# A graph layer on one core: dense work dealt by another rule, ending one group of 16 chunks later

## The chip, the cores and the metric

The kernel runs on one core of a Trainium2 chip. The time is device microseconds of one execution; lower is better. A time is the median of several runs, and a profile is one further execution with the profiler on.

## The reference

```python
h = jnp.maximum(_layernorm(x, axis=-1), 0.0)           # x: 12500 nodes x 128
xs = h[src]                                            # 200000 edges, sorted by dst
msgs = zeros
for i in range(4):                                     # four edge types
    msgs += where(edge_type == i, xs @ W[i] + b[i], 0)
return x + segment_sum(msgs, dst, num_segments=12500)
```

Each of the 200,000 edges takes the normalized row of its source node, multiplies it by the weights of the edge's type and adds the result to the row of its destination. The edges are sorted by destination, and the low destinations have by far the most edges.

## The kernel before, in words

The 200,000 edges are cut into 1,563 chunks of 128. They are treated in two ways.

*The first 568 chunks are dense.* Their edges go to some 1,700 destinations. For these the kernel counts, with matmuls of one-hots, how many edges of each type lead from each source node to each destination (`count`), and then multiplies the table of all 12,500 normalized rows by these counts (`multiply`). Up to 31 units of three destinations make a batch, and there are 19 batches, the first of 22. Counting a batch takes a matmul for each slot (`pt<-o,o`, L1099; 1,069 slots in all), for which VectorE makes two one-hots (L1066 and L1074), and ScalarE takes the sums out (L1107). Multiplying is called a pass: it reads the table in 33 blocks of three by 128 rows (`hs`, loaded on SyncE's queue into five buffers, L1195) and issues matmuls into `pa` (L1211). The first pass reads the table `htab`, with three parts for each row and three matmuls for 128 rows, and writes a packed table `dtab` on the way (`keep`, L1181 to L1183). Every later pass reads `dtab` with two matmuls for 128 rows, one of which needs counts that ScalarE has decoded (`dec`, L1167). While batch n is counted, batch n - 1 is passed over, a little behind.

*The other 995 chunks are sparse.* A gather on GpSimd's queue (L591) fetches the 128 source rows of a chunk from `htab`, VectorE makes a one-hot of key and type (`oh`, L609), and three matmuls of L644 add the rows up. A group is 16 chunks; once for a group, counts and sums are weighed with the weights (`weigh`, L661 to L670), and VectorE adds the outcome to a ring of destinations (L733), from which finished blocks are put out (`put_out`, `leave`, L766 and L771). The first three groups (RAW) are treated apart, from rows of `x`; their last steps (`raw_steps`, L702 to L715) are popped in group 3. Groups 3 to 59 have 16 chunks each, and 8, 12, 8, 4 and 3 chunks follow as groups 60 to 64. The gathers of group g + 1 are issued in group g, into ten buffers of two chunks, so a gather can run at most 20 chunks ahead of TensorE.

*The order on the engines is written out by hand* for TensorE, VectorE and ScalarE. In the main loop `sum_up` yields eight times in a group, after every two chunks, and at each yield dense steps are issued until their share of the whole reaches `pace(gi, part)`:

```python
for j, part in enumerate(sum_up(t0, g, *now, gi >= FULL)):
    while work and spent < pace(gi, part):
        spent = next(work, None)
```

`pace` gives every group the same number of columns, sparse columns (`columns`) and dense ones together. The dense total is the sum over slots and passes of estimated columns; `dense_work` adds up the same estimates as steps are issued. In the group in which the dense work is found to be over, its buffers are released, the finished rows of the dense destinations are fetched and leave in the group behind it (`leaves`), the blocks that are due from that group on are fetched ahead as well (`late`), and the sums are checked (`check_all`, which multiplies by an all-ones tile). `FULL` is 60, `LEAD` is 3, `NB` is 392.

Of the kernel before, what the change touches and what calls it, by code (L numbers as in the profile page):

```python
# [35 lines left out]
F32 = mybir.dt.float32  # L36
BF16 = mybir.dt.bfloat16
# [7 lines left out]
ALU = mybir.AluOpType  # L45
# [5 lines left out]
P = 128  # L51
EPS = 1e-5
UN = 3
G = 16
SG = 4
WIN = 32
# [10 lines left out]
SETTLE = 0.5  # L67
# [5 lines left out]
LEAD = RAW  # L73
# [4 lines left out]
DECS = 4  # L78
UP = 4096.0
PARTS = 2.05  # L80


@with_exitstack
def kernel(
# [10 lines left out]
    nc = tc.nc  # L95
    N, D = x.shape
    E = src.shape[0]
    NT, _, DO = w.shape
    assert D == P and DO == P
    NW = -(-N // P)  # L100
# [41 lines left out]
    for k in range(max(segs[0][4])):  # L142
        for s in (0, 1, 2, 3) if k == 0 else (1, 0, 2, 3):
            n = sum(c > k for c in segs[s][4])
# [9 lines left out]
    FULL = (TM - sum(ends_in)) // G  # L154
# [13 lines left out]
    alone = [(k, d) for k in range(0, max(segs[0][4]), 2) for d in range(FIRST) if segs[0][4][d] > k]  # L168
# [10 lines left out]
    batches = []  # L179
# [15 lines left out]
    def slots_of(u):  # L195

        got = []
        u = list(zip(u, (1.0, 256.0, 65536.0)))
        if u[0][0] is not None and u[0][0][1] >= FIRST:
            d = u[0][0][1]  # L200
            size = size_of(d)
            got += [(slot_at(k, d), None) for k in range(chunks_of(d, size))]
            del u[:size]
        for v, by in u:
            if v is not None:
                k, d = v
                got += [(slot_at(i, d), by) for i in (k, k + 1) if i < segs[0][4][d]]
        return got

    NSLOTS = sum(len(slots_of(u)) for vs in batches for u in vs)  # L210
    NB = NW * NT


# [209 lines left out]
    nc.gpsimd.iota(iota_i, pattern=[[1, P]], base=0, channel_multiplier=0)  # L423
    iota_b = const.tile([P, P], BF16, name="iota_b")
    nc.vector.tensor_copy(iota_b, iota_i)
    iota_1 = const.tile([P, P], BF16, name="iota_1")
    nc.vector.tensor_single_scalar(iota_1, iota_b, 1.0, op=ALU.add)
    iota_f = prep.tile([P, KR], F32, name="iota_f", bufs=1)
    nc.vector.tensor_copy(iota_f, iota_i[:, :KR])
    iota_d = prep.tile([P, NB], I32, name="iota_d", bufs=1)  # L430
# [19 lines left out]
    nc.vector.memset(ones_h, 1.0)  # L450
    ones_b = const.tile([P, 3], BF16, name="ones_b")
    nc.vector.memset(ones_b, 1.0)
    ones = const.tile([P, P], F32, name="ones")
    nc.vector.memset(ones, 1.0)
    eps = const.tile([P, 1], F32, name="eps")

    zero = const.tile([P, 1], F32, name="zero")
# [103 lines left out]
    marks = []  # L561
# [88 lines left out]
    def weigh(t0, g, oh, sb, last):  # L650
        win = window_of(C0 + t0)

        def bank(own):
            settle(owed)
            to = y_ps.tile([P, G * WIN], F32, name="py") if own else x_ps.tile([P, G * WIN], F32, name="pt")
            return to[:, : G * win].rearrange("p (g n) -> p g n", g=G)

        ohv = oh.rearrange("p g (t n) -> p g t n", t=NT)
        pc = bank(False)
        for t in range(NT):  # L660
            nc.tensor.matmul(  # L661
                pc[t * CG : (t + 1) * CG, :g, :], three, ohv[:, :g, t, :], start=True, stop=True, tile_position=(0, t * CG)
            )
        cnt = spool.tile([P, G * WIN], BF16, name="cnt", bufs=1)[:, : G * win].rearrange("p (g n) -> p g n", g=G)
        nc.scalar.copy(cnt[:, :g], pc[:, :g])  # L665
        yield True
        py = bank(not last)
        nc.tensor.matmul(py[:, :g, :], b128, cnt[:, :g, :], start=True, stop=False)
        for t in range(NT):
            nc.tensor.matmul(py[:, :g, :], wsb[:, t, :], sb[0][:, :g, t, :], start=False, stop=(t == NT - 1))  # L670
        adds.extend(ring_adds(t0, g, lambda i: py[:, i, :], win))
        yield True
# [174 lines left out]
    def check_all():  # L847
        nc.vector.tensor_single_scalar(bad[:, 4:5], most, MANY + 0.5, op=ALU.is_gt)
        many = const.tile([P, 3], F32, name="many")
        nc.vector.tensor_reduce(many[:, 0:1], bad, AX.X, ALU.add)  # L850
        nc.vector.tensor_copy(many[:, 1:2], seen)
        nc.vector.tensor_copy(many[:, 2:3], held)
        pb = x_ps.tile([P, 3], F32, name="pt")
        nc.tensor.matmul(pb, ones, many, start=True, stop=True)
        sums_ok = const.tile([P, 3], F32, name="sums_ok")
        nc.vector.tensor_single_scalar(sums_ok[:, 0:1], pb[:, 0:1], 0.5, op=ALU.is_gt)
        nc.vector.tensor_single_scalar(sums_ok[:, 1:2], pb[:, 1:2], 3.0 * E0, op=ALU.not_equal)
        nc.vector.tensor_single_scalar(sums_ok[:, 2:3], pb[:, 2:3], float(E0), op=ALU.not_equal)
        nc.vector.tensor_reduce(flag, sums_ok, AX.X, ALU.max)
# [14 lines left out]
    def make_slots(dix):  # L874
# [44 lines left out]
        for u0, n, _, _, caps in segs:  # L919
            i = 0  # L920
# [52 lines left out]
        def unpack(a, z, shared):  # L973
# [5 lines left out]
            marks.append(nc.vector.tensor_copy(hkT[:, a:z], hk).ins)  # L979
            lo = dix.tile([P, 512], I32, name="lo")[:, :n]  # L980
            nc.vector.tensor_single_scalar(lo, xi, 255, op=ALU.bitwise_and)
            marks.append(nc.vector.tensor_copy(loT[:, a:z], lo).ins)
            if shared:
                by = byT[:, a - FIRST : z - FIRST]
                nc.vector.tensor_single_scalar(xi, xi, 768, op=ALU.bitwise_and)
# [56 lines left out]
    def count(now, room):  # L1042
# [18 lines left out]
        def make(n):  # L1061
            at = before + n
            o1 = op1.tile([P, SLOTS, P], BF16, name="o1")
            o2 = o2s[:, at % SETS]
            for k, (i, s, by, first, last) in enumerate(sets[n]):
                one = nc.vector.tensor_scalar(o2[:, k, :NB], iota_n, hkT[:, s : s + 1], None, ALU.is_equal)  # L1066
                if k == 0 and at >= SETS:
                    held_by(one, released[at - SETS], "a set of slots has been counted as a whole")
                if by == 1.0:
                    one = nc.vector.tensor_scalar(o1[:, k], iota_1, loT[:, s : s + 1], None, ALU.is_equal)  # L1070
                else:
                    if by is None:
                        by = byT[:, s - FIRST : s - FIRST + 1]
                    one = nc.vector.tensor_scalar(o1[:, k], iota_1, loT[:, s : s + 1], by, ALU.is_equal, ALU.mult)  # L1074
                yield o1[:, k], o2[:, k], one.ins

        making = []
# [183 lines left out]
    def columns(gi):  # L1261

        K = NT * window_of(C0 + starts[gi])
        return sizes[gi] * (3 * max(64, K) + 5 * K)

    def pace(gi, part):

        last = FULL - 1
        if gi >= last:
            return 2.0  # L1270
        own = [columns(i) for i in range(LEAD, last)]
        a_group = (dense_columns() + sum(own)) / len(own)
        n = gi - LEAD
        if n < 0:
            return 0.0
        return ((n + part) * a_group - sum(own[:n]) - part * own[n]) / dense_columns()

    def dense_columns():
        return NSLOTS * float(NB) + sum(3 * len(vs) * (PARTS if i else 3.0) for i, vs in enumerate(batches)) * NW * NT

    def begin(n):
        now = [batches[n], None]
# [2 lines left out]
    def dense_work():  # L1285


        a_slot = float(NB)
        alone_slot = 3.5 * NB
        a_node = NW * NT  # L1290
        total = dense_columns() + sum(len(slots_of(u)) for u in batches[0]) * (alone_slot - a_slot)
        gone = 0.0
        before = None
        coming = None
        for n, vs in enumerate(batches + [None]):
            steps, led = {}, {}
            now = None
            if n == 1:
                end_raws()
            if vs:  # L1300
                now, first = coming or begin(n)
                coming = None
                steps[first] = sum(len(slots_of(u)) for u in vs) * (a_slot if before else alone_slot)
            if before:
                passed = multiply(before)
                steps[passed] = 3 * len(before[0]) * a_node * (PARTS if before[0] is not batches[0] else 3.0)
                led = {passed: SETTLE if before[0] is batches[1] else BEHIND}
            done = {st: 0.0 for st in steps}
            opened = 0 if before else DECS - 1
            while done:  # L1310
                while opened < DECS - 1 and (
                    vs is None or done.get(first, 1.0) >= led[passed] - BEHIND * (DECS - 1 - opened) / (DECS - 1)
                ):
                    next(passed)
                    opened += 1
                st = min(done, key=lambda st: done[st] + led.get(st, 0.0))
                part = next(st, None)
                if part is None:
                    del done[st]
                    gone += steps[st]  # L1320
                    if vs and st is first and n + 1 < len(batches):
                        coming = begin(n + 1)
                        next(coming[1])
                else:
                    done[st] = part
                    yield (gone + sum(done[st] * steps[st] for st in done)) / total
            before = now
        settle(sds)

# [308 lines left out]
    with tc.If(rv > 0):  # L1638
        with tc.tile_pool(name="slow", bufs=1) as slow, tc.tile_pool(name="slow_ps", bufs=1, space=PSUM) as slow_ps:
# [7 lines left out]
            nc.gpsimd.iota(part_i, pattern=[[0, 1]], base=NW * P + P, channel_multiplier=1)  # L1647
            part_f = slow.tile([P, 1], F32, name="part_f")
            nc.vector.tensor_copy(part_f, part_i)
            before = slow.tile([P, P], F32, name="before")  # L1650
            nc.gpsimd.affine_select(
                out=before, in_=ones, compare_op=ALU.is_gt, fill=0.0, base=0, pattern=[[1, P]], channel_multiplier=-1
# [106 lines left out]
```

## Time and profile before

| | |
|---|---|
| median of 3 runs | 1355.36 us (1352.13 to 1356.22) |
| the profiled execution | 1360.44 us |
| its span in the profile | 1358.7 us |
| busy: PE, ACT, DVE, POOL | 1243.1, 1066.8, 999.0, 977.8 us |
| gathers L591 | 947 |
| dense matmuls: L1211, L1099 | 3822, 1069 |

PE is TensorE, PEld its weight loads, ACT ScalarE, DVE VectorE, POOL GpSimd and SP SyncE. Rows by stretch hold, for each engine, the busy time and the number of instructions, then the granted share of TensorE's clock, the share of time in which the DMA engines were busy, and the rate in GB/s.

### The profile page before, as it was taken

Reading aid. Unit: us, or ns where it says so; the run is one execution under the profiler, and the core shown is the slowest. Engines: PE = TensorE matmul, PEld = TensorE weight load, DVE = VectorE, ACT = ScalarE, POOL = GpSimd, SP = SyncE. Lnnn points to the kernel's source line nnn. Section 1 sums busy time; section 2 is a strip of 40 time slices with the busy share of each in tenths; the row PEclk is TensorE's granted clock in tenths of the full one; section 3 lists DMA queues with packets and bytes.
Section 4 is the critical chain, followed back from the end, with each engine's and each line's share of the span. In section 5 each row is a group of like instructions: output and inputs, shape, how many; then the busy total and the mean of one; then the engine's idle time right before and its main releaser. Section 6 shows DMA issues by size and latency. Waiting matters only on the chain.

```text
span 1358.7 us, 30461 instructions
## 1 busy us (share of the span) xinstructions
PE 1243.1 (91%) x9232; PEld 872.8 (64%) x9232; DVE 999.0 (74%) x5139; ACT 1066.8 (79%) x1815; POOL 977.8 (72%) x1024
## 2 busy tenths in 40 slices
PE   5888877999999999999999999999999999998964
PEld 1445654777677766777777676666676666666743
DVE  8996568868888897888776867677676758773552
ACT  6887544889889888898988988888897978886710
POOL 7637463777777777777777777777777777777774
PEclk8885887999999999999999999999999999999977
DMA  7653596888788888888888888887877878778842
GB/s 243 216 204 86 176 338 216 244 272 266 243 256 259 250 255 241 249 257 265 256 259 254 267 249 257 248 246 246 273 227 238 265 214 261 235 234 281 267 122 62
DMA packets 184630, 322.56 MB, mean 237 GB/s; under 512 B 30243, under 2 KB 82524, under 8 KB 184460
## 3 DMA queue, kind: packets, MB, share of 16 engines
q1 hardware_dynamic: 132716, 214.63, 49.0%
q0 software_dynamic: 46992, 96.30, 26.0%
q10 hardware_dynamic: 4752, 9.64, 1.8%
q8 instruction: 73, 1.20, 0.4%
q14 instruction: 97, 0.79, 0.2%
HBM read 294.78 MB, written 25.67 MB: 236 GB/s over the span
## 4 chain that ended last, share of the span: by engine, by line
PE 65%; DMA 12%; DVE 6%; ACT 6%; issue 6%; POOL 4%; DVEq 0%; SPq 0%; ACTq 0%; POOLq 0%
PE pa L1211 35%; PE pt L1099 9%; PE py L670 7%; DMA hm<-htab,srcT 7%; PE ps L644 5%; POOL hm L591 4%; DMA dtab<-dec 2%; DMA hs<-dtab 2%; ACT dec L1167 2%; PE pt L1235 2%; ACT counts L1107 1%; PE ps L702 1%; DVE o L1074 1%; DVE o L1066 1%; PE pt L952 1%
## 5 line engine op out<-in xcount | busy, mean ns | idle before, releaser
L591 POOL DMA_INDIRECT hm<-htab,srcT x947 | 924.3, 976 | 342.1 <-issue 202.5
L1167 ACT ACTIVATE dec<-counts 128x1116 fp32r<-128x1116 uint8 (+1 forms) x594 | 672.2, 1152 | 9.9 <-PE pa L1211 9.0
L1066 DVE TENSOR_SCALAR o<-iota_n,hkT 128x392 bf16<-128x392 f16 x1069 | 354.4, 331 | 180.2 <-PE pt L1099 177.4
L1211 PE MATMUL pa<-dec,hs 128*128 128x372 f32 x1764 | 480.8, 380 | 0.0
L1211 PE MATMUL pa<-counts,hs 128*128 128x372 fp8e4 (+1 forms) x2058 | 435.0, 324 | 22.6 <-DMA hs<-htab 13.8
L1211 PEld LDWEIGHTS pa<-dec,hs 128*128 128x128 f32 x1764 | 309.5, 188 | 41.6 <-issue 0.5
L1107 ACT CAST counts<-pt 128x396 int32<-128x396 f32 x580 | 285.5, 510 | 50.1 <-PE pt L1099 26.2
L1099 PE MATMUL pt<-o,o 128*128 128x396 bf16 x1069 | 285.9, 342 | 15.8 <-ACT counts L1107 9.5
L1211 PEld LDWEIGHTS <-hs 128*128 128x128 f16 (+1 forms) x2058 | 189.6, 98 | 143.1 <-issue 19.4
L644 PE MATMUL ps<-oh,hm 128*128 128x72 bf16 (+7 forms) x2841 | 186.9, 201 | 32.3 <-DMA hm<-htab,srcT 30.9
L1074 DVE TENSOR_SCALAR o<-iota,loT,byT 128x128 bf16<-128x128 bf16 x647 | 216.3, 334 | 0.0
L733 DVE TENSOR_TENSOR ring<-ring,py 128x18 f32 (+6 forms) x912 | 159.0, 174 | 73.1 <-PE py L670 24.1
L644 PEld LDWEIGHTS <-hm 128*128 128x128 f16 x2841 | 136.9, 100 | 103.9 <-DMA hm<-htab,srcT 41.4
L634 ACT ACTIVATE sb<-ps 128x288 f32<-128x288 f32 (+8 forms) x237 | 101.8, 430 | 126.3 <-PE py L670 101.3
L609 DVE TENSOR_SCALAR oh<-iota_b,keyT 128x72 bf16<-128x72 bf16 (+7 forms) x947 | 163.0, 260 | 25.6 <-PE ps L644 24.4
L670 PE MATMUL py<-sb,wsb 128*128 128x288 f32 (+6 forms) x456 | 121.1, 409 | 0.0
L1099 PEld LDWEIGHTS <-o 128*128 128x128 bf16 x1069 | 80.4, 99 | 60.6 <-issue 17.5
L1074 DVE TENSOR_SCALAR o<-iota,loT 128x128 bf16<-128x128 bf16 x422 | 116.7, 277 | 0.0
L670 PEld LDWEIGHTS py<-sb,wsb 128*128 128x128 f32 x456 | 83.3, 193 | 20.7 <-issue 0.3
L575 POOL DMA_INDIRECT hx<-in_x_dram,srcT x48 | 48.0, 1001 | 23.8 <-issue 9.5
L665 ACT CAST cnt<-pt 128x288 bf16<-128x288 f32 (+10 forms) x62 | 25.5, 412 | 39.5 <-PE pt L661 33.6
L509 ACT ACTIVATE h<-hm,nmrt,rstdt 128x128 f32<-128x128 f32 x98 | 42.1, 489 | 0.9 <-DVE mvt L492 0.8
(250 smaller groups left out, 717.8 us busy)
## 6 DMA issues: line engine op xcount, KB each, us to landing
hs<-dtab SPq DMA_DIRECT2D x576, 288.0 KB
hm<-htab,srcT POOLq DMA_INDIRECT x947
htab<-h SPq DMA_DIRECT2D x32, 288.0 KB
hs<-htab SPq DMA_DIRECT2D x32, 288.0 KB
dtab<-dec ACTq DMA_DIRECT2D x32, 288.0 KB
xo<-in_x_dram SPq DMA_DIRECT2D x23, 256.0 KB
out_dram<-xo SPq DMA_DIRECT2D x23, 256.0 KB
hm<-in_x_dram SPq DMA_DIRECT2D x18, 192.0 KB
```

The lines of the kernel that those rows point to most:

```text
L591: one = nc.gpsimd.indirect_dma_start(out=hm[:, (i - h0) * D3 : (i - h0 + 1) * D3], out_offset=None, in_=htab, in_offset=bass.IndirectOffse ...
L609: nc.vector.tensor_scalar(oh[:, i, :], iota_b[:, :K], keyf[:, at : at + 1], None, ALU.is_equal)
L634: nc.scalar.activation(sb[0][:, i0:i1].rearrange("p g t n -> p g (t n)"), ps[:, : i1 - i0, :], AF.Copy, scale=1.0 / UP)
L644: nc.tensor.matmul(ps[:, i - i0, :], rows(i, c), oh[:, i, :], start=(c == 0), stop=(c == 2))
L670: nc.tensor.matmul(py[:, :g, :], wsb[:, t, :], sb[0][:, :g, t, :], start=False, stop=(t == NT - 1))
L733: nc.vector.tensor_tensor(to, to, of(i), ALU.add)
L1066: one = nc.vector.tensor_scalar(o2[:, k, :NB], iota_n, hkT[:, s : s + 1], None, ALU.is_equal)
L1074: one = nc.vector.tensor_scalar(o1[:, k], iota_1, loT[:, s : s + 1], by, ALU.is_equal, ALU.mult)
L1099: one = nc.tensor.matmul(pb, o1, o2, start=first, stop=last)
L1107: lambda i=i, pb=pb: nc.scalar.copy(counts[:, :, i * NT : (i + 1) * NT], pb.rearrange("p (b t) -> p b t", t=NT))
L1167: nc.scalar.activation(decoded[n][:, : j1 - j0, :nv].rearrange("p j (m v) -> p j m v", m=3), by_digit[:, j0:j1, : nu * NT * 4].rearrange(" ...
L1211: nc.tensor.matmul(to if c == 1 and not first else to.rearrange("p (m v) -> p m v", m=3), left, right, start=(j == 0 and c == 0), stop=(js ...
```

## The change

`pace` and `dense_work` now use the same two estimates, written as functions of how much of a step is done. A slot of the first batch, and of the first half of batch 2 (which is counted with no pass beside it), stands for 3.5 times the columns of another slot (`ALONE`). In the old rule only `dense_work` knew this, and for the first batch alone. The first pass stands for 4.4 instead of 3.0 columns for a node and unit (`FIRST_PASS`); the later ones keep 2.05. Group 3, with the steps of the raw groups, counts as 20,000 columns fuller (`RAW_WORK`; the sparse columns of a group are some 7,000 to 12,000). The dense work is dealt over groups 3 to 59 instead of 3 to 58 (`last`). Three smaller edits go with it: the constant `iota_1` is gone, and `loT` holds the value less one instead; the all-ones tile is made where it is used, not at the start; and `cnt` has room for 26 columns a chunk instead of 32.

```diff
+FIRST_PASS = 4.4
+ALONE = 3.5
+RAW_WORK = 20000.0
...
-    iota_1 = const.tile([P, P], BF16, name="iota_1")
-    nc.vector.tensor_single_scalar(iota_1, iota_b, 1.0, op=ALU.add)
...
-    ones = const.tile([P, P], F32, name="ones")
-    nc.vector.memset(ones, 1.0)
...
-        cnt = spool.tile([P, G * WIN], BF16, name="cnt", bufs=1)[:, : G * win].rearrange("p (g n) -> p g n", g=G)
+        cnt = spool.tile([P, G * KM // NT], BF16, name="cnt", bufs=1)[:, : G * win].rearrange("p (g n) -> p g n", g=G)
...
         pb = x_ps.tile([P, 3], F32, name="pt")
+        ones = outp.tile([P, P], F32, name="ones", bufs=1)
+        nc.vector.memset(ones, 1.0)
         nc.tensor.matmul(pb, ones, many, start=True, stop=True)
...
-            marks.append(nc.vector.tensor_copy(loT[:, a:z], lo).ins)
+            marks.append(nc.vector.tensor_single_scalar(loT[:, a:z], lo, -1.0, op=ALU.add).ins)
...
-                    one = nc.vector.tensor_scalar(o1[:, k], iota_1, loT[:, s : s + 1], None, ALU.is_equal)
+                    one = nc.vector.tensor_scalar(o1[:, k], iota_b, loT[:, s : s + 1], None, ALU.is_equal)
...
     def pace(gi, part):
 
-        last = FULL - 1
+        last = FULL
         if gi >= last:
             return 2.0
-        own = [columns(i) for i in range(LEAD, last)]
+        own = [columns(i) + (RAW_WORK if i == LEAD else 0.0) for i in range(LEAD, last)]
...
+    def counting_columns(n, part):
+
+        alone = 1.0 if n == 0 else SETTLE if n == 2 else 0.0
+        return sum(len(slots_of(u)) for u in batches[n]) * NB * (part + (ALONE - 1.0) * min(part, alone))
+
+    def passing_columns(n, part):
+        return 3.0 * len(batches[n]) * (PARTS if n else FIRST_PASS) * NW * NT * part
+
     def dense_columns():
-        return NSLOTS * float(NB) + sum(3 * len(vs) * (PARTS if i else 3.0) for i, vs in enumerate(batches)) * NW * NT
+        return sum(counting_columns(n, 1.0) + passing_columns(n, 1.0) for n in range(len(batches)))
...
-        a_slot = float(NB)
-        alone_slot = 3.5 * NB
-        a_node = NW * NT
-        total = dense_columns() + sum(len(slots_of(u)) for u in batches[0]) * (alone_slot - a_slot)
+        total = dense_columns()
...
-                steps[first] = sum(len(slots_of(u)) for u in vs) * (a_slot if before else alone_slot)
+                steps[first] = lambda part, n=n: counting_columns(n, part)
...
-                steps[passed] = 3 * len(before[0]) * a_node * (PARTS if before[0] is not batches[0] else 3.0)
+                steps[passed] = lambda part, n=n: passing_columns(n - 1, part)
...
-                    yield (gone + sum(done[st] * steps[st] for st in done)) / total
+                    yield (gone + sum(steps[st](done[st]) for st in done)) / total
```

More of the change, by code (lines that the diff above doesn't have):

```diff
@@ L208, in slots_of @@
         return got
-    NSLOTS = sum(len(slots_of(u)) for vs in batches for u in vs)
     NB = NW * NT
@@ L1073, in make @@
                         by = byT[:, s - FIRST : s - FIRST + 1]
-                    one = nc.vector.tensor_scalar(o1[:, k], iota_1, loT[:, s : s + 1], by, ALU.is_equal, ALU.mult)
+                    one = nc.vector.tensor_scalar(o1[:, k], iota_b, loT[:, s : s + 1], by, ALU.is_equal, ALU.mult)
                 yield o1[:, k], o2[:, k], one.ins
@@ L1319, in dense_work @@
                     del done[st]
-                    gone += steps[st]
+                    gone += steps[st](1.0)
                     if vs and st is first and n + 1 < len(batches):
@@ L1649 @@
             nc.vector.tensor_copy(part_f, part_i)
+            ones = slow.tile([P, P], F32, name="ones")
+            nc.vector.memset(ones, 1.0)
             before = slow.tile([P, P], F32, name="before")
```

## The prediction

> **What bounds the kernel now.** I read the page first, for span, chain and slices.
>
> ```profile
> span 1358.7 us, 30461 instructions
> ...
> POOL 7637463777777777777777777777777777777774
> ...
> PE 65%; DMA 12%; DVE 6%; ACT 6%; issue 6%; POOL 4%; DVEq 0%; SPq 0%; ACTq 0%; POOLq 0%
> ```
>
> The chain of waits names PE for 65% of the span. The POOL slices say something else: the same digit from the eighth slice to the last but one, whatever PE does. An engine that is fed by others does not run so evenly. To decide, I cut the span at the groups of 16 chunks that the loop walks through, at the first L644 matmul of a group, and asked for the busy times of each stretch (columns: length; busy time and count of PE, PEld, DVE, ACT, POOL; granted clock; DMA share; GB/s).
>
> ```profile
> 112.10:152.10 40.00, 33.32 (x201) 25.70 (x201) 21.41 (x96) 30.36 (x85) 23.59 (x25) 0.63 0.26 72
> 152.10:176.30 24.20, 20.72 (x194) 15.91 (x193) 18.49 (x84) 12.10 (x31) 15.78 (x15) 0.93 0.92 311
> 176.30:206.60 30.30, 22.36 (x195) 16.13 (x193) 17.56 (x79) 13.40 (x33) 17.20 (x18) 0.89 0.98 342
> 206.60:243.20 36.60, 28.54 (x173) 17.17 (x172) 31.48 (x152) 18.94 (x38) 15.52 (x15) 0.72 0.62 196
> 243.20:282.10 38.90, 38.27 (x314) 27.86 (x311) 29.47 (x165) 35.91 (x51) 29.71 (x31) 1.00 0.89 276
> 282.10:718.30 436.20, 427.30 (x3416) 309.54 (x3415) 356.03 (x1853) 384.63 (x608) 332.55 (x341) 1.00 0.84 255
> 718.30:1288.80 570.50, 548.23 (x4149) 390.59 (x4147) 398.29 (x2077) 478.25 (x729) 433.60 (x450) 1.00 0.82 251
> 1288.80:1344.80 56.00, 36.14 (x241) 24.80 (x240) 21.80 (x120) 7.47 (x18) 42.59 (x45) 0.71 0.40 106
> 1344.80:1358.70 13.90, 5.17 (x41) 3.98 (x39) 4.00 (x19) 1.17 (x3) 0.00 (x0) 0.75 0.13 37
> ```
>
> These are groups 3, 4, 5, 6, then 7 and 8, then 9 to 30, 31 to 58, and 59 to 64, and the rest after the last gather. The matmuls of L644 (three for each chunk, 48 for a group) show the cut: 22 groups, then 28.
>
> ```profile
> 282.10:718.30 436.20, 59.79 (x1057) 45.21 (x1058) 1.00 0.84 255
> 718.30:1288.80 570.50, 93.72 (x1344) 67.14 (x1343) 1.00 0.82 251
> ```
>
> From 282.1 to 1288.8 POOL issues 341 + 450 = 791 gathers in 1006.7 us, one in **1.273 us**, so 20.4 us for a group. In the stretch without dense work, 1288.8 to 1344.8, it is 56.0/45 = 1.24 us: hardly faster, with PE busy 65% and the DMA share halved. So POOL paces the kernel by itself from 282 on, and the end is its last gather plus 13.9 us. PE needs 427.3/22 = 19.4 us of work for a group, 98% of its stretch, then 548.2/28 = 19.6 us: it is just under POOL's pace.
>
> Before 282.1 POOL does lose time: 25 + 15 + 18 + 15 + 31 = 104 gathers take 170.0 us, where 104 x 1.273 = 132.4 would do. **37.6 us** are lost, and who took them stands in the waits of 112 to 282:
>
> ```profile
> POOL hm L591 <- PE ps L644: 25.7, 12, 5.0
> ...
> POOL hm L591 <- PE pt L1099: 12.7, 10, 3.4
> ```
>
> 38.4 us in 22 waits for PE. The row buffers hold 20 chunks; a gather waits until PE has multiplied the chunk 20 places earlier, and PE is late because dense work is queued between the sparse matmuls. That is the place the change touches.
>
> **The change part by part.** *Where the dense work goes.* Dense matmuls of the trace in these stretches, passes (L1211), then counts (L1099):
>
> ```profile
> 112.10:152.10 40.00, 2.24 (x18) 1.73 (x18) 0.63 0.26 72
> 152.10:176.30 24.20, 17.27 (x119) 11.57 (x117) 0.93 0.92 311
> 176.30:206.60 30.30, 18.05 (x119) 11.59 (x117) 0.89 0.98 342
> 206.60:243.20 36.60, 12.11 (x61) 7.61 (x60) 0.72 0.62 196
> 243.20:282.10 38.90, 30.49 (x162) 20.91 (x162) 1.00 0.89 276
> 282.10:718.30 436.20, 287.96 (x1486) 197.83 (x1484) 1.00 0.84 255
> 718.30:1288.80 570.50, 360.56 (x1864) 247.91 (x1864) 1.00 0.82 251
> ```
>
> ```profile
> 112.10:152.10 40.00, 9.69 (x28) 2.81 (x28) 0.63 0.26 72
> 152.10:176.30 24.20, 4.28 (x12) 1.20 (x12) 0.93 0.92 311
> 176.30:206.60 30.30, 4.67 (x13) 1.34 (x13) 0.89 0.98 342
> 206.60:243.20 36.60, 12.94 (x41) 3.63 (x41) 0.72 0.62 196
> 243.20:282.10 38.90, 7.38 (x30) 1.88 (x28) 1.00 0.89 276
> 282.10:718.30 436.20, 124.32 (x493) 34.74 (x493) 1.00 0.84 255
> 718.30:1288.80 570.50, 122.59 (x455) 34.75 (x454) 1.00 0.82 251
> ```
>
> I worked the rule of `pace` through by arithmetic, step by step. With the old constants it gives 18, 117, 117, 60 and 72 + 90 passes and 28, 12, 13, 41 and 24 + 4 counts for groups 3 to 8, which is what these rows show. With the new ones it gives 0, 54, 90, 81, 69, 0 passes and 13, 19, 9, 9, 9, 27 counts, and from group 9 to 59 some 69 passes and 19 counts in each; the last pass ends with group 59, not 58.
>
> *Group 3.* It loses 15 counts and 18 passes. The passes are 2.2 us. A count is worth 0.35 us by PE's row (9.69/28). VectorE, which must first make two one-hots for it, needs 0.33 + 0.33 us:
>
> ```profile
> L1066 DVE TENSOR_SCALAR o<-iota_n,hkT 128x392 bf16<-128x392 f16 x1069 | 354.4, 331 | 180.2 <-PE pt L1099 177.4
> ...
> L1074 DVE TENSOR_SCALAR o<-iota,loT,byT 128x128 bf16<-128x128 bf16 x647 | 216.3, 334 | 0.0
> L733 DVE TENSOR_TENSOR ring<-ring,py 128x18 f32 (+6 forms) x912 | 159.0, 174 | 73.1 <-PE py L670 24.1
> ...
> L609 DVE TENSOR_SCALAR oh<-iota_b,keyT 128x72 bf16<-128x72 bf16 (+7 forms) x947 | 163.0, 260 | 25.6 <-PE ps L644 24.4
> ```
>
> So 15 counts are 5.2 to 10.0 us; the other work of this group, which goes through ACT (30.4 of 40.0 us busy) as well, stays. I take 40 - 9 = 31 us, nearer to PE's row: group 4 starts at 143 and not at 152. If ACT holds the group up, nothing but 2 us goes.
>
> *Groups 4 to 7.* The old groups 4 and 5 took 54.5 us for 238 passes with everything that lay among them: 0.229 us for a pass. At that price 90, 81 and 69 passes are 20.6, 18.5 and 15.8 us; 54 passes are 12.4 us, and with 9 counts made alone at 0.665 us and 10 beside passes at 0.25 us (124.32/493), group 4 is 20.9 us. All are at or under POOL's 20.4, so POOL sets them: 4 x 20.4 = 82. The price holds a DMA share of 0.92 to 0.98; spread over four groups the first pass asks for less, so it is no lower bound. Its loads on SP's queue and its stores on ACT's move along with it; both queues lose by it, since the same bytes have longer.
>
> *Group 8.* 27 counts alone on VectorE, 27 x 0.665 = 18.0 us, and beside them 16 one-hots at 0.26 and 16 additions to the ring at 0.174: 25 us on VectorE. Group 9 then starts at 143 + 82 + 25 = 250 where it was 282.1: **32 us** earlier, and POOL, which is 20 chunks ahead in both, as well. It would be 37.6 if POOL never waited.
>
> *From group 9 on.* 51 groups take 983 counts and 3,528 passes, where 50 took 947 and 3,348: 0.33 counts and 2.2 passes more for a group. By these rows a count is 0.25 us and a pass 0.194 us, so PE needs 0.51 us more: 19.9 us for groups 9 to 30, 20.1 from 31 on, against POOL's 20.4. PE's idle time there that is not waiting for a gather (8.9 us in 22 groups, 0.4 for each) stays: 20.3 and 20.5. That is even with POOL. It costs between nothing and 0.3 us for a group; I take 2 us in all.
>
> *The end.* After group 59 come 35 chunks, 44.6 us at POOL's pace, in which PE is busy two thirds. The tables' final rows leave one group later, in group 61, still covered by POOL's gathers there; the output block due at group 59 is now loaded when it is put out instead of ahead, and its load waits for a buffer. On VectorE the additions to the ring and the next one-hots are queued behind that. It costs nothing as long as VectorE catches up within 20 chunks; without that cover it is bounded by the gathers of the group it lies in, 12 x 1.273 = 15 us.
>
> *The constant.* One 128x128 constant less, the comparison shifted by one in `loT` (an instruction changed, none added), the all-ones tile filled later, a smaller `cnt`: a few instructions of a fraction of a microsecond each, beside POOL's pace. Nothing.
>
> The sum against the profiled execution: 1360.4 - 32 + 2 = 1330. The runs shown have their median 5.1 us below it (1355.4), so **1325** for the median.
>
> **Rivals.** *PE becomes the bound after group 9.* For: 98% busy, an estimate that comes out even. Against: its stretch 718 to 1288 still had 22 us idle. At 0.3 us over POOL, 51 groups give back 15: 1340.
>
> *PE's clock falls in the thin groups.* Granted clock and PE's busy share go together in the rows: 1.00 at 98%, 0.72 at 78%, 0.71 at 65% (1288.8 to 1344.8). The thinned groups would have PE busy some 16 of 20 us. At a clock of 0.5, 20.72 us of group 4 before, scaled to 90 passes of 119 and from 0.93 to 0.5, are 29 us: groups 4 to 8 take about 130 us, group 9 starts near 273, and 9 us are gained: 1346. The page "TensorE: Matmul & The Clock Gate" of the Trainium skill, Part 1, states a rule against this change: the clock is halved by default and after an idle window of about 3.4 us, and only sustained activity restores it. The rows between 0.63 and 0.93 agree with a mix of the two. By that rule spreading matmuls thinner is not free.
>
> *Slower: PE's queue gets longer than POOL's pace hides.* If a group of 9 to 59 took x us, group 59 ends at 250 + 51x, and 15 gathers, those beyond the 20 that the buffers hold, and the tail follow, 19 + 14 us. That exceeds 1358.7 from x = 21.1. Dense work now lies one group nearer to the end, so 21.3 would mean 1369 of span, 1366 as a median. For: PE waits on VectorE and ACT in the middle of a queue in order. Against: it needs 0.8 us over my sum in each group.
>
> *It does not do what it says.* If group 3 to 8 are held by table and slots, not by dense work, nothing moves: 1355. The POOL waits on PE rows speak against it.
>
> **How the numbers follow.** The forecast has 0.62, with its own range from 1317 (all 37.6 us) to 1334 (group 3 hardly shorter, 7 us); PE bound 0.18; the clock 0.09; slower 0.08; no change 0.03. From 1316 to 1345 leaves out half of the clock's case, the slower one and no change. A measurement of this kernel tells about 0.3%, 4 us, from no change. Faster: 0.62 + 0.18 + 0.09, less 0.01 for the clock's far end, 0.88; same 0.04; slower 0.08.
>
> **What would show it.** Right: the first sparse matmul of group 9 near 250; POOL's gathers 1.27 us apart from about there to the end, its waits on PE in the first groups down from 38 to below 15 us; the last gather near 1313 and some 14 us after it. Wrong: gaps between gathers after 250 that PE releases (the bound moved), a granted clock under 0.7 with long matmuls in groups 4 to 8, or a group 3 still near 40 us.

## The result, and the profile after

| | before | after |
|---|---|---|
| median | 1355.03 us (1352.13 to 1356.22, 4 runs) | 1334.38 us (1333.87 to 1334.58, 4 runs) |
| the profiled execution, its span | 1360.44, 1358.7 us | 1334.58, 1332.9 us |

The ratio is 0.9844, with a 95% interval of 0.9821 to 0.9866: 20.6 us less, where 30 were forecast. In the experiments below ratios count, because in the series of e5 to e8 and of e9 to e12 every kernel, the one before included (1634.9 and 1633.5 us), took 20% longer; each ratio is to the kernel before in the same series.

The page of the changed kernel: span, then POOL's slices, then the chain.

```profile
span 1332.9 us, 30465 instructions
...
POOL 7627677777777777777777777777777777777774
...
PE 74%; DVE 9%; DMA 8%; ACT 5%; issue 2%; DVEq 0%; SPq 0%; POOL 0%; POOLq 0%; ACTq 0%
```

The even row of sevens has grown to the left: before, slices five to seven were 4, 6 and 3, and now they are 6, 7 and 7. The chain gives POOL 0% now and PE 74%, although POOL's pace is what the kernel runs at (e4 below shows it). The stretches of the changed kernel, cut at the first sparse matmul of a group: groups 3, 4, 5, 6, 7, 8, then 9 to 30, 31 to 58, 59, and from 60 to just behind the last gather. The columns are those of the prediction. In the changed kernel the lines L589, L607, L632, L642, L731 and L769 are what L591, L609, L634, L644, L733 and L771 were.

```profile
111.60:147.90 36.30, 31.23 (x169) 25.98 (x169) 12.49 (x61) 23.04 (x65) 23.40 (x24) 0.50 0.30 79
147.90:166.70 18.80, 15.81 (x138) 10.89 (x137) 17.32 (x83) 12.78 (x35) 14.54 (x15) 0.85 0.44 119
166.70:190.10 23.40, 17.83 (x164) 12.96 (x162) 19.07 (x94) 10.52 (x27) 17.92 (x19) 0.85 1.01 355
190.10:211.30 21.20, 16.12 (x156) 12.27 (x155) 12.69 (x60) 8.68 (x21) 14.71 (x16) 0.92 0.99 334
211.30:231.50 20.20, 14.98 (x141) 10.71 (x139) 14.11 (x63) 7.48 (x19) 14.98 (x15) 0.92 0.98 341
231.50:251.00 19.50, 13.07 (x97) 8.87 (x97) 18.95 (x106) 11.87 (x26) 15.05 (x15) 0.77 0.51 160
251.00:698.20 447.20, 438.20 (x3465) 316.31 (x3464) 363.11 (x1879) 392.68 (x612) 341.21 (x348) 0.99 0.83 254
698.20:1265.60 567.40, 556.35 (x4234) 398.19 (x4233) 412.43 (x2162) 493.68 (x759) 431.58 (x446) 1.00 0.84 256
1265.60:1285.10 19.50, 19.50 (x148) 14.27 (x147) 6.16 (x34) 14.26 (x18) 14.86 (x16) 1.00 0.86 272
1285.10:1319.90 34.80, 24.55 (x179) 19.50 (x178) 15.61 (x87) 4.88 (x12) 25.72 (x28) 0.82 0.46 121
```

Group 9 starts at 251.0 where it started at 282.1: 31.1 us. Groups 4 to 8 take 18.8 to 23.4 us, 20.6 on average, about POOL's 20.4. The last gather ends at 1319.0, where 1313 was forecast, 13.9 us before the end of the span, as before. From group 9 to 58 PE is busy 98% of the time, and POOL still issues a gather every 1.278 us, (348 + 446) in 1014.6 us. The waits of POOL for PE in the stretch 111 to 251 (total, times, longest):

```profile
POOL hm L589 <- issue: 21.3, 70, 0.3
...
POOL hm L589 <- PE ps L642: 10.4, 6, 3.9
...
POOL hm L589 <- PE pt L1099: 3.0, 10, 0.3
```

38.4 us have become 13.4. Both figures hold usual gaps: POOL stands 0.3 us before every gather, also where it waits for nothing. Without these, the 22 waits of before are 31.8 us. A single wait that the prediction left out, 5.4 us without its gap, belongs to them:

```profile
POOL hm L591 <- ACT sb L634: 5.7, 1, 5.7
```

That makes 37.2 us lost, against 37.6 by the count of gathers. After the change 8.6 us are left, and by the same count the 104 gathers of groups 3 to 8 take 139.4 us where 132.4 would do. What is left stands before four gathers that wait for sparse matmuls. The three longest (start, duration, idle time before it and who ended it), of which the first two are in group 3:

```profile
142.88 0.94 POOL L589 DMA_INDIRECT hm<-htab,srcT  x1 [3.86 <-PE ps L642]
...
147.72 0.94 POOL L589 DMA_INDIRECT hm<-htab,srcT  x1 [2.64 <-PE ps L642]
...
199.15 0.95 POOL L589 DMA_INDIRECT hm<-htab,srcT  x1 [2.22 <-PE ps L642]
```

### The profile page after: what moved, and what is told of

It reads as the page before. It is cut to its first block, busy times and chain, and to the rows that moved or that the text cites. A ratio compares the mean times of both kernels' runs of the same rounds, so it can differ in the third digit from the quotient of the medians.

```text
span 1332.9 us, 30465 instructions
## 1 busy us (share of the span) xinstructions
PE 1233.0 (93%) x9232; PEld 873.9 (66%) x9232; DVE 996.0 (75%) x5138; ACT 1065.4 (80%) x1815; POOL 980.2 (74%) x1024
## 4 chain that ended last, share of the span: by engine, by line
PE 74%; DVE 9%; DMA 8%; ACT 5%; issue 2%; DVEq 0%; SPq 0%; POOL 0%; POOLq 0%; ACTq 0%
PE pa L1211 40%; PE pt L1099 11%; PE py L668 8%; PE ps L642 6%; DMA hs<-dtab 3%; ACT dec L1167 2%; PE pt L1235 2%; DVE ring L731 2%; DMA dtab<-dec 2%; DVE o L1074 2%; PE ps L700 1%; PE pt L952 1%; DVE o L1066 1%; DMA out_dram<-xo 1%; ACT counts L1107 1%
## 5 line engine op out<-in xcount | busy, mean ns | idle before, releaser
L589 POOL DMA_INDIRECT hm<-htab,srcT x947 | 927.3, 979 | 313.3 <-issue 195.9
L1066 DVE TENSOR_SCALAR o<-iota_n,hkT 128x392 bf16<-128x392 f16 x1069 | 356.2, 333 | 188.0 <-PE pt L1099 181.2
L1074 DVE TENSOR_SCALAR o<-iota_b,loT,byT 128x128 bf16<-128x128 bf16 x647 | 214.7, 332 | 0.0
L731 DVE TENSOR_TENSOR ring<-ring,py 128x18 f32 (+6 forms) x912 | 158.6, 174 | 54.9 <-issue 14.9
L632 ACT ACTIVATE sb<-ps 128x288 f32<-128x288 f32 (+8 forms) x237 | 102.1, 432 | 115.5 <-PE py L668 94.5
L642 PE MATMUL ps<-oh,hm 128*128 128x72 bf16 (+7 forms) x2841 | 178.6, 200 | 5.5 <-DMA hm<-htab,srcT 3.7
L642 PEld LDWEIGHTS <-hm 128*128 128x128 f16 x2841 | 136.9, 100 | 69.9 <-issue 18.3
L607 DVE TENSOR_SCALAR oh<-iota_b,keyT 128x72 bf16<-128x72 bf16 (+7 forms) x947 | 164.4, 263 | 18.0 <-PE ps L642 18.0
L1074 DVE TENSOR_SCALAR o<-iota_b,loT 128x128 bf16<-128x128 bf16 x422 | 116.2, 275 | 0.0
```

The costliest lines, as they stand in the source:

```text
L589: one = nc.gpsimd.indirect_dma_start(out=hm[:, (i - h0) * D3 : (i - h0 + 1) * D3], out_offset=None, in_=htab, in_offset=bass.IndirectOffse ...
L607: nc.vector.tensor_scalar(oh[:, i, :], iota_b[:, :K], keyf[:, at : at + 1], None, ALU.is_equal)
L632: nc.scalar.activation(sb[0][:, i0:i1].rearrange("p g t n -> p g (t n)"), ps[:, : i1 - i0, :], AF.Copy, scale=1.0 / UP)
L642: nc.tensor.matmul(ps[:, i - i0, :], rows(i, c), oh[:, i, :], start=(c == 0), stop=(c == 2))
L731: nc.vector.tensor_tensor(to, to, of(i), ALU.add)
L1074: one = nc.vector.tensor_scalar(o1[:, k], iota_b, loT[:, s : s + 1], by, ALU.is_equal, ALU.mult)
```

## Experiments

The theory: POOL's own pace sets the time, and the change gains what POOL no longer waits in groups 4 to 8, because the first pass is dealt thinner. Rivals: the later end is what pays; the fuller weight of group 3; the small edits; or PE sets the pace and POOL only follows.

**e4: half the passes.** The second matmul of later passes is left out.

```diff
-                    if not first:
+                    if not first and j == 0:
                         todo.append((1, j, hs.bitcast(F32R)[:, j - j0, D // 2 :], decoded[j // DS][:, j % DS, :nv]))
```

> The changed kernel without the second matmul of nearly every later pass (1,746 of the 1,764 that read decoded counts are left out; the decoding stays), so the output lacks that part. PE then has some 6 us less in each group after the eighth. Theory (POOL's own pace of 1.27 us for a gather sets the rest): the time falls by no more than 8 us, to 1325 to 1334 us, with gathers still 1.27 us apart. Rival (PE's queue sets the pace after group 9, and POOL only follows it): 1050 to 1290 us, with gathers closer together.

Measured: ratio 0.9837 (0.9805 to 0.9870), 1335.7 us, the same as the changed kernel and a little above the expected range. Its page, PE's and POOL's busy time:

```profile
PE 1033.7 (77%) x7486; PEld 635.0 (48%) x7486; DVE 994.4 (74%) x5138; ACT 1062.4 (80%) x1815; POOL 978.1 (73%) x1024
...
POOL 7627676777777777777777777777777777777774
```

Its stretch of groups 9 to 58, and who waits there:

```profile
253.50:1263.20 1009.70, 801.13 (x5993) 483.33 (x5992) 772.80 (x4037) 882.51 (x1369) 768.83 (x791) 0.93 0.83 256
```

```profile
PEld L642 <- DMA hm<-htab,srcT: 223.9, 236, 3.5
PE ps L642 <- DMA hm<-htab,srcT: 175.5, 190, 3.4
```

PE lost some 190 us of work in these groups and the time did not move: 791 gathers in 1009.7 us, 1.276 us each, and PE now stands waiting for the gathered rows. So POOL paces the kernel in these groups, PE is just within it, and a chain that names PE for 74% of the span does not say that PE's work is worth cutting.

**e1: the later end alone.** The kernel before with `last = FULL`.

```diff
-        last = FULL - 1
+        last = FULL
```

> The kernel before, with the dense work dealt to group 59 instead of 58 and nothing else. If the gain is POOL's waits for row buffers in groups 4 to 8 (theory), little moves: by the rule's arithmetic groups 3 to 8 get 18, 108, 117, 69, 66, 84 passes where they had 18, 117, 117, 60, 72, 90, so group 9 still starts near 280: 1352 to 1357 us. If the later end is what pays (rival: fewer dense columns in every group, and work in a group that had none), most of the gain is here: 1335 to 1342 us.

Measured: 1.0053 (1.0035 to 1.0071), 1363.9 us. No gain: the rival, that the later end pays by itself, falls. It is even half a per cent slower, which neither side expected (1352 to 1357 us at most). The profile has POOL's early waits as they were (42.7 us for PE in groups 3 to 8, 38.4 before), and its execution was the fastest of the seven, 1359.0 us, so it can't show where the 5.7 us went. That stays open.

**e3: the old end with the thin start.** The reverse: the changed kernel with `last = FULL - 1`.

> The changed kernel with its dense work ending in group 58 again. Theory: groups 3 to 8 keep nearly the same dense work (0, 54, 90, 90, 60, 0 passes), so the gain stays but for 1 or 2 us: 1334 to 1338 us; PE has 0.4 us more in each of 50 groups and runs at POOL's pace or just over it. Rival (the later end pays): 1347 us or more.

Measured: 0.9903 (0.9874 to 0.9931), 1344.1 us. Between the two expectations: by the medians some 0.6% or 8 us of the change's gain need the later end, at least four times what I had put. The stretch of groups 9 to 58 and POOL's waits in it:

```profile
256.10:1284.90 1028.80, 1010.63 (x7778) 726.19 (x7777) 774.89 (x4037) 898.68 (x1381) 778.38 (x802) 1.00 0.84 256
```

```profile
POOL hm L589 <- PE ps L642: 17.9, 42, 1.8
```

A group takes 1028.8/50 = 20.6 us against 1014.6/50 = 20.3 in the changed kernel, and POOL waits for a sparse matmul for up to 1.8 us, where no wait of the changed kernel exceeds 0.3 in this stretch. So the two parts are no sum. PE's busy time for a group from 9 to 58 was 19.5 us in the kernel before, is 19.9 in the changed one and 20.2 here, where POOL needs 20.4 and PE has some 0.4 us of idle time besides. By these numbers PE has room with the thick start, and the later end gives nothing; with the thin start the work moved to the later groups fills PE to POOL's pace, and the room of one more group decides whether it overflows.

**e2: the first pass at its old weight.** `FIRST_PASS = 3.0`.

> The changed kernel with the first pass at its old 3.0 columns. Theory: groups 4 to 6 get 72, 117, 105 passes instead of 54, 90, 81, the batch-2 count stands in group 7, and group 9 starts 10 to 16 us later: 1344 to 1350 us. Rival (the fuller weight of group 3, not of the first pass, does it): 1334 to 1337 us.

Measured: 0.9932 (0.9907 to 0.9958), 1348.1 us, in the middle of the expectation. Group 9 starts at 266.6, 15.6 us later, and POOL waits for PE in groups 3 to 8 grow from 13.4 us to

```profile
POOL hm L589 <- PE ps L642: 13.0, 9, 3.4
POOL hm L589 <- PE pt L1099: 13.0, 11, 3.7
```

By the medians this one number carries 12 of the 21 us. The third new weight, `ALONE` for the counts of batch 2, was not varied by itself.

**e5: no weight for group 3.** `RAW_WORK = 0.0`.

> The changed kernel with RAW_WORK at 0, so group 3 gets its full share of dense work again (18 passes, 28 counts; then 81, 81, 90, 24, 30 passes). Theory: group 3 ends 4 us later, POOL waits for it once, the rest of the first pass stays thin: 1 to 5 us more than the changed kernel, a ratio of 0.985 to 0.989 to the kernel before. Rival (the weight of group 3 is what pays): 0.994 or more.

Measured: 0.9866 (0.9803 to 0.9930), where the changed kernel in the same series had 0.9827 (0.9760 to 0.9893). As the theory has it, and not what the rival needs; but the two intervals overlap, so the size is not settled. In the traces of e5 to e12 a gather starts only every 1.55 to 1.60 us on average from the first to the last (1.29 in the changed kernel's profile above). POOL's own pace doesn't set the time there, so these runs say less of it than e1 to e4 do.

**e6: the small edits alone**, with the old pacing.

> The kernel before with the constant, the shifted comparison, the later all-ones tile and the smaller cnt, and with the old pacing. Theory: no difference, ratio 0.998 to 1.002, POOL's waits in groups 4 to 8 still some 37 us. Rival (the space or the shorter start is worth something): under 0.997.

Measured: 0.9995 (0.9960 to 1.0029). If they are worth anything in time, it is less than this run can tell (0.3 to 0.4%, some 5 us).

**e7 and e10: eleven row buffers.** What is left of POOL's early waits is for buffers.

```diff
-    hpool = mid.enter_context(tc.tile_pool(name="rows", bufs=10))
+    hpool = mid.enter_context(tc.tile_pool(name="rows", bufs=11))
```

> The changed kernel with 11 row buffers for the gathers instead of 10, so POOL can be 22 chunks ahead; the space that the small edits free makes room for it. Theory (POOL's waits for a row buffer are what is left, 8.6 us in groups 5 to 8): they fall by 3 to 6 us and the time with them, ratio 0.980 to 0.983. Rival (the row buffers are not what those gathers wait for): no difference, 0.984.

> Eleven row buffers again, since the chip of the first try paused all engines every few us. Theory (POOL still waits 8.6 us for a buffer): 3 to 6 us less than the changed kernel beside it. Rival (buffers gain nothing, what they hold ahead is lost elsewhere): within 2 us of it or more.

Measured: 0.9879 (0.9815 to 0.9943) and 0.9885 (0.9862 to 0.9909), where the changed kernel beside them had 0.9827 and 0.9818 (0.9783 to 0.9853). Slower by 0.5 to 0.7%; the intervals of e9 and e10 lie apart, those of e8 and e7 overlap. The 8.6 us of the expectations are not where they put them: 5.9 lie in group 3, and only 2.7 in groups 5 to 8. They also missed that the same buffers load the node blocks while the table is made. The first gathers of the two kernels (start, duration, idle time and releaser), first the changed kernel (e9), then eleven buffers (e10):

```profile
108.44 0.94 POOL L589 DMA_INDIRECT hm<-htab,srcT  x1 [16.24 <-DMA htab<-h]
```

```profile
115.88 1.08 POOL L589 DMA_INDIRECT hm<-htab,srcT  x1 [21.29 <-ACT ints L1010]
```

The first gather comes 7.4 us later here, and 6.6 us later in e7 than in e8, so the table phase, whose order is not written out by hand, came out otherwise. That this is the whole loss was not tested, and whether the buffers themselves gain anything in groups 5 to 8 these runs don't tell.

**e8 and e9: the changed kernel again**, as the measure for the others.

> The changed kernel again, on the chip of this comparison, as the measure for the others: ratio 0.982 to 0.987.

> The changed kernel, as the measure for the runs beside it: ratio 0.982 to 0.987 to the kernel before.

0.9827 and 0.9818: the gain repeats.

**e11: thinner still.** `FIRST_PASS = 6.0`, `RAW_WORK = 30000.0`.

> The changed kernel with FIRST_PASS 6.0 and RAW_WORK 30000: 0, 27, 63, 72, 63, 69 passes and 6, 23, 7, 7, 7, 3 counts in groups 3 to 8, and 0.6 counts more in each later group. Theory: the early waits fall to some 5 us, but PE, already even with POOL, goes over its pace from group 9 on, and POOL waits for it there: 0 to 6 us more than the changed kernel. Rival (thinner is simply better while POOL paces): 3 to 6 us less.

Measured: 0.9810 (0.9784 to 0.9835) against 0.9818 beside it. The same, at the lower edge of the theory. But the rival's 3 us less lie inside the interval as well, so the run doesn't decide between them. No version tried here beats the changed kernel beyond the noise.

**e12: the late block fetched ahead.** The block due at group 59 is loaded with the others again.

```diff
-            late = [(ja, jb) for (ja, jb, _), i in zip(flushes, goes) if i >= gi]
+            late = [(ja, jb) for (ja, jb, _), i in zip(flushes, goes) if i >= gi - 1]
```

> The changed kernel with the output block due at group 59 fetched ahead with the others again, so VectorE's 5.6 us wait for its load in group 61 goes. Theory (POOL's gathers cover that group): within 2 us of the changed kernel. Rival (the wait reaches the end through TensorE, which stands 2.9 us behind it): 3 to 6 us less.

Measured: 0.9815 (0.9787 to 0.9843), the same as 0.9818, though the interval doesn't rule out 3 us. The wait is there in the changed kernel, on VectorE in group 61:

```profile
1304.46 0.69 DVE L769 TENSOR_TENSOR xo<-pt,xo 128x512 f32<-128x512 f32 x1 [5.55 <-DMA xo<-in_x_dram]
```

and POOL's gathers go on beside it at gaps of 0.3 us until 1319.0, so there they cover it, as the prediction had put it.

## Why the prediction was right, step by step

*POOL paces, and its early waits are the gain*: shown, by e4 and e2. The waits fell as forecast, to 13.4 us. The time alone wouldn't have shown it: 1334.4 us lies at the far end of the forecast's own range (1317 to 1334), and nearer to the 1340 of the rival in which PE is the bound than to the 1325 of the forecast. It is e4 that decides between the two.

*Group 9 near 250*: measured 251.0, and this closeness is luck: two of its terms missed by some 5 us each, in opposite directions. Group 3 takes 36.3 us, not 31: only 3.7 us of the nine went. The passes and 15 counts that left it took 6.4 us off PE's rows (2.24, and 9.69 less 5.50), but PE's busy time fell by 2.1 us only, from 33.3 to 31.2. The matmuls that stay got longer, and the granted clock of the stretch fell from 0.63 to 0.50. The matmuls of the raw groups in it, before and after (mean ns behind the busy time):

```profile
L702 PE MATMUL ps<-ohf,hx 128*128 128x48 f32 x32 | 4.7, 299 | 1.7 <-ACT sbr L703 1.4 <-ACT sb L634 0.3
```

```profile
L700 PE MATMUL ps<-ohf,hx 128*128 128x48 f32 x32 | 7.0, 405 | 0.0
```

This fits the slower clock, which the prediction named as a rival for groups 4 to 8 and not for group 3. How much of the group's length it explains was not tested. Group 8 takes 19.5 us, not 25. VectorE is busy for 18.95 us of it, though POOL issues at its usual gaps of 0.3 us all through, so that VectorE sets its length is not shown. The 25 us were too much because VectorE's instructions overlap in the profile: the four kinds that I added up are busy 9.35 (L1066), 8.54 (L1074), 2.68 (L607) and 3.31 us (L731) in that stretch, 23.9 together. A sum of counts times mean durations, which is how I priced group 8 and the counts of group 3, counts the overlaps twice. Groups 4 to 7 take 83.6 us against 82.

*A thinner first pass asks less of the DMA engines*: right for group 4 alone (a share of 0.44), wrong for groups 5 to 7. There the share is 0.98 to 1.01 at 334 to 355 GB/s; a block of the first pass takes 2.3 us (10 blocks in 23.4 us), as in the old group 5 (13 in 30.3), and PE waits 11.0 us for these loads in groups 3 to 8. At 2.3 us for a block of 9 passes a group of 20.4 us has room for almost 80 passes, and the new weight deals 90, 81 and 69 to groups 5 to 7. The Trainium skill's "DMA: Bandwidth & Descriptors", under Bandwidth, gives about 358 GB/s as the limit of one core between HBM and SBUF, and in the same place 425 GB/s for one large load with the neighbouring core idle. The 355 GB/s measured here lie at the first figure; no run here shows which limit holds this pass.

*From group 9 on*: the 31.1 us are not kept whole. From the first matmul of group 9 to the end of the last gather it took 1062.7 us and takes 1068.0. Of these 5.3 us, 3.2 are POOL's lead: its first gather of group 10 started 1.6 us before the first matmul of group 9 and starts 1.6 us after it now, where the prediction took the lead as equal ("as well"). The other 2.1 are its pace, 1.277 us a gather for 1.275. I had put 2 us for the whole term.

*From one execution to the median*: the largest part of the miss. The profiled execution before lay 5.1 us above the median that was shown and 4.2 above the slowest of those runs; the one after lies 0.2 above its median. In spans the gain is 25.8 us, in medians 20.6. I carried the offset over as if the changed kernel would have it too. But the kernel before spreads over 1352 to 1362 us in its runs (here and beside e1 to e4), and the changed one over 0.7 us in its four. Some of the lost time read out of that profile may be that execution's own; with one trace of the kernel before, that is not shown. So 9.4 us were missed: 4.2 in the terms above, 5.2 in this step.

*The rivals.* PE did not become the bound with the new end, but e3 shows that it is only just so. The clock did fall, to 0.85 to 0.92 in groups 4 to 7 and 0.77 in group 8, not to 0.5; POOL waited there for 2.7 us in all beyond its usual gaps, so it cost little. It doesn't simply follow PE's busy share, as the prediction read it: it is 0.50 in group 3 with PE busy 86%, and 0.92 in group 7 with 74%. (Before, it was 0.63 in group 3 with 83%, a row that the prediction showed and did not count.) The later end alone, which I had not listed as a cause of its own, is worth nothing without the thin start and some 8 us with it.

## What to carry to other kernels

Look for the engine with an even row before you believe the chain: an engine that issues at the same interval in stretch after stretch may pace the kernel, and then what it lost before it reached that interval is the gain to be had; leaving out half of another engine's work settles it in one run. Take the usual gaps out of the waits before you add them up. When work is dealt by estimates, give the step that waits for transfers a weight by what bounds it; thinning the start only pays if the later groups still fit under the pace. Set a profiled execution against the spread of the runs before you take its lost time as the kernel's.

## What the runs showed of the hardware

One indirect gather of 128 rows occupies POOL for a median of 0.95 us, and the next starts 0.30 us later. The stretches of the kernel before hardly differ: 0.97 us on average from 282.1 to 1288.8, with a DMA share of 0.82 to 0.84, and 0.95 from 1288.8 to 1344.8, with 0.40.

In the trace of e9 a gather is as long as ever, 0.97 us on average, but pauses stand between the gathers:

```profile
601.20 0.95 POOL L589 DMA_INDIRECT hm<-htab,srcT  x1 [0.30 <-issue]
603.68 0.94 POOL L589 DMA_INDIRECT hm<-htab,srcT  x1 [1.54 <-remote]
604.93 1.02 POOL L589 DMA_INDIRECT hm<-htab,srcT  x1 [0.30 <-issue]
...
612.76 0.94 POOL L589 DMA_INDIRECT hm<-htab,srcT  x1 [1.73 <-remote]
```

From 300 to 1500 us there are 185 such pauses of more than 0.9 us, most of them every fourth gather, with a median of 1.4 us. The rows shown name no engine of this core ("remote"), but for 150 of the 185 the profile names PE, and all 185 stand before the first of the two gathers that share a row buffer, which is where POOL waits for a buffer. What makes the buffers come free later there was not settled. That the chip pauses its engines, as the expectation of e10 has it, is not shown.
